# A two-layer graph network on one core: issue order written out by hand, masks on GpSimd, a per-node stage in small portions

## The chip, the core and the metric

The kernel runs on one core of a Trainium2 chip. A core has five engines that run side by side and wait for one another through semaphores: TensorE (PE, matmuls; its weight loads are listed apart as PEld), VectorE (DVE), ScalarE (ACT), GpSimd (POOL) and SyncE (SP, which here only issues DMAs). The metric is the device time of one execution in microseconds (us), the median over several runs.

## What is computed

There are N = 3327 nodes with D = 64 features and a 0/1 adjacency of 3327 x 3327. Both layers start with a layer norm and a relu and are added to their input. Cut to what matters:

```python
# layer 0: h = relu(layernorm(x)); c = 1 / r**2
left, right = x_t @ w_att[:D], x_t @ w_att[D:]             # x_t = logmap0(h)
adj_att   = sigmoid(left[:, None] + right[None, :] + b) * adj
x_local   = logmap(h[:, None], h[None, :], c)              # a vector for each pair
support_t = einsum('ij,ijd->id', adj_att, x_local)
x = x + proj(expmap(h, support_t, c), c)
# layer 1: h = relu(layernorm(x)); support = h @ weight
mask = (adj != 0); rank = cumsum(mask, axis=1)
k    = minimum(deg, 100); pos = rank - (deg - k)           # deg = rank[:, -1]
w    = mask * where(pos > 0, 0.5 ** (k - pos), 0)          # the last 100 neighbours
x = x + w @ support + bias
```

The vector of a pair is a combination of h of node i and h of node j, with a factor that depends on one scalar of the pair. So the kernel forms, for each pair, a scalar q by matmul, two gelus of it, a sigmoid, and their product with the adjacency; one matmul then sums over j. Layer 1 needs for each pair the number of neighbours behind j in row i; the weight is a power of two of that number.

## The kernel before

Nodes are padded to 26 blocks of 128. The first stage works per node (layer norm, norms, factors, 16-bit splits, and the transposes that give `ju` and `jz`, the two operands of the pair scalars). Then come the **pair stages**: four strips of columns i (8, 8, 6 and 4 blocks), and in each strip a loop over the blocks j from 25 down to 0. A **round** handles one j (in the last strip two), so that a tile has 128 rows j and 1024 columns i (768 in the third strip). There are 26 + 26 + 26 + 13 = 91 rounds. A round does, in the order of the code:

- one DMA of adjacency, `ad`, on SP's queue;
- `mask` from `ad` by a comparison on DVE (L824);
- **the count**: matmuls with the constants `ca` and `cb` (L829, L830) add to `pc`, which stays in PSUM for the whole strip; a first matmul of one row (L808) sets the offset. ACT (L834) or DVE (L836) reads `pc` into `behind`, an 8-bit array that is kept. DVE does every second read in the first strip and every fourth one later;
- tanh on ACT for the sigmoid (L841), then on DVE `sg = (sg + 1) * ad` (L842, the first product);
- four 16-bit matmuls per tile into `pq` (L847, L848), two gelus on ACT, from PSUM into SBUF (L850) and in place (L851), then on DVE `s = (s + WD) * sg` (L852, the second product);
- f32 matmuls that add to `po` over the strip (L855).

At the end of a strip `po` is copied out (L861), turned by PE (L865) and copied by ACT into `agg`. Then `post`, the **node stage** of that strip, is a generator: each `next(steps)` in the rounds of the following strip issues a piece of it. It uses DVE, ACT for squares and a tanh, and three calls of `rsqrt`, each a bit trick with three Newton steps on DVE. Its last values, `s2`, are layer 1's right side. In the node stage POOL adds the bias to `x_sb` (L771). `in_range` tests that the inputs are in the range of this fast path and sets `flag`.

**Layer 1** decodes `behind` for each j into 16-bit weights `wt` (two of five on ACT, L887, the others on DVE, L889) and multiplies with `s2` into seven PSUM tiles (L894). The node stage of the last strip runs beside it, so the last four blocks come last: 28 matmuls, then a copy out, small f32 matmuls with the layer's weight (L917), an add (L919) and a DMA for each of the seven tiles.

The order of instructions on each engine isn't the order of the code: a scheduler takes all instructions that the code traces and orders them for each engine by its own cost model, within their dependencies and buffers.

Of the kernel before, what the change touches and what calls it, by code (L numbers as in the profile page):

```python
# [14 lines left out]
I32 = mybir.dt.int32  # L15
# [15 lines left out]
JH = 13  # L31

# [35 lines left out]
CNT = 127.0  # L68
# [367 lines left out]
def fast(ctx, tc, x, adj_t, r, w_att, b_att, weight, bias, out, flag):  # L436
# [33 lines left out]
    q0_c = column(Q0, "q0_c")  # L470
    ident = const.tile([P, P], F32, name="ident")
# [3 lines left out]

    cb = const.tile([P, P], BF16, name="cb")
    ca = const.tile([P, P], BF16, name="ca")
    G.memset(ca, -1.0)
    G.affine_select(out=cb, in_=ca, compare_op=ALU.is_gt, fill=0.0, base=0,
                    pattern=[[-1, P]], channel_multiplier=1)  # L480
    G.affine_select(out=cb, in_=cb, compare_op=ALU.not_equal, fill=CNT, base=0,
                    pattern=[[-1, P]], channel_multiplier=1)
    G.tensor_sub(ca, ca, cb)
    row1 = const.tile([1, P], BF16, name="row1")
    G.memset(row1, 1.0)
    rowc = const.tile([1, 512], BF16, name="rowc")
    G.memset(rowc, MAX_NEIGH - CNT)

# [13 lines left out]
    def rsqrt(pool, y, v, n):  # L502

        t = pool.tile([P, n], F32, name="rs_t")
        g = pool.tile([P, n], F32, name="rs_g")
        V.tensor_scalar(t.bitcast(I32), v.bitcast(I32), 1, None, op0=ALU.logical_shift_right)
        V.tensor_scalar(y.bitcast(I32), t.bitcast(I32), -1.0, float(0x5F3759DF), op0=ALU.mult, op1=ALU.add)
        V.tensor_scalar(g, v, -0.5, None, op0=ALU.mult)
        for _ in range(3):
            V.tensor_mul(t, y, y)  # L510
            V.tensor_mul(t, t, g)
            V.scalar_tensor_tensor(y, t, 1.5, y, op0=ALU.add, op1=ALU.mult)

    def wide(t, n):
# [4 lines left out]
    x2, bal, balm, nrm, left, right = (  # L519
        const.tile([P, NB], F32, name=n) for n in ("x2", "bal", "balm", "nrm", "left", "right"))  # L520
# [6 lines left out]

    post_pool = ctx.enter_context(tc.tile_pool(name="post", bufs=1))
# [3 lines left out]
    with tc.tile_pool(name="pre", bufs=1) as pre:  # L532
# [17 lines left out]
        rsqrt(pre, y, v, NB)  # L550
# [58 lines left out]
        rsqrt(pre, yr, x2c, NB)  # L609
# [37 lines left out]
        V.tensor_scalar(balm, bal, MIN_NORM, None, op0=ALU.max)  # L647
        V.tensor_scalar(maxnorm, absr, 1.0 - EPS_BALL, None, op0=ALU.mult)
# [11 lines left out]
    def in_range():  # L660

        st = post_pool.tile([P, 4], F32, name="st")
        t1 = post_pool.tile([P, NB], F32, name="st1")
        V.tensor_mul(t1, nrm, node)
        V.tensor_reduce(st[:, 0:1], t1, AX.X, ALU.max)
        V.scalar_tensor_tensor(t1, x2, c_c, t1, op0=ALU.mult, op1=ALU.mult)
        V.tensor_reduce(st[:, 1:2], t1, AX.X, ALU.max)
        V.tensor_mul(t1, bal, node)
        V.tensor_reduce(st[:, 2:3], t1, AX.X, ALU.max)
        V.tensor_reduce(st[:, 3:4], t1, AX.X, ALU.min)  # L670
        V.tensor_scalar(st[:, 3:4], st[:, 3:4], -1.0, None, op0=ALU.mult)
        pf = ps.tile([P, P], F32, name="pq", bufs=2)
# [3 lines left out]
        pf = ps.tile([P, P], F32, name="pq", bufs=2)  # L676
# [12 lines left out]
    def post(agg, b0, nb):  # L689
# [11 lines left out]
        sa, t0, t1, k, y2, u2, xy, rn = (small(n) for n in ("sa", "t0", "t1", "k", "y2", "u2", "xy", "rn"))  # L701
        u, w, dt = big("u"), big("w"), big("dt")
        V.tensor_mul(t0, nrm[:, bs], balm[:, bs])
        V.tensor_mul(t1, bal[:, bs], t0)
        V.tensor_mul(dt, hs, v)
        yield
        V.tensor_reduce(xy, dt, AX.X, ALU.add)
        V.scalar_tensor_tensor(sa, xy, m2c, agg[:, :, D], op0=ALU.mult, op1=ALU.add)
        V.tensor_mul(sa, sa, t0)
        yield  # L710
        V.tensor_mul(u, v, wide(t1, nb))
        yield
        V.tensor_mul(w, hs, wide(sa, nb))
        yield
        V.tensor_sub(u, u, w)
        A.activation(dt, u, AF.Square)

        V.tensor_mul(xy, xy, t1)
        V.tensor_mul(sa, sa, x2[:, bs])
        V.tensor_sub(xy, xy, sa)  # L720
        yield

        V.tensor_reduce(u2, dt, AX.X, ALU.add)
        V.tensor_scalar(t0, u2, MIN_NORM, None, op0=ALU.max)
        yield
        rsqrt(pool, rn, t0, nb)
        V.tensor_mul(t0, t0, rn)
        V.reciprocal(t1, balm[:, bs])
        V.scalar_tensor_tensor(t0, t0, sqc, t1, op0=ALU.mult, op1=ALU.mult)
        A.activation(k, t0, AF.Tanh)  # L730
        yield
        V.scalar_tensor_tensor(k, k, absr, rn, op0=ALU.mult, op1=ALU.mult)

        V.tensor_mul(y2, u2, k)
        V.tensor_mul(y2, y2, k)
        V.tensor_mul(xy, xy, k)
        V.tensor_scalar(xy, xy, m2c, -1.0, op0=ALU.mult, op1=ALU.mult)
        V.tensor_scalar(xy, xy, 1.0, None, op0=ALU.add)
        V.scalar_tensor_tensor(t0, y2, c_c, xy, op0=ALU.mult, op1=ALU.add)
        V.scalar_tensor_tensor(t1, y2, c2_c, x2[:, bs], op0=ALU.mult, op1=ALU.mult)  # L740
        V.tensor_add(t1, t1, xy)
        V.tensor_scalar(t1, t1, MIN_NORM, None, op0=ALU.max)
        V.reciprocal(t1, t1)
        V.tensor_mul(t0, t0, t1)
        V.tensor_mul(k, k, bal[:, bs])
        V.tensor_mul(k, k, t1)
        yield
        V.tensor_mul(w, hs, wide(t0, nb))
        yield
        V.tensor_mul(u, u, wide(k, nb))  # L750
        yield
        V.tensor_add(u, u, w)
        A.activation(dt, u, AF.Square)
        yield

        V.tensor_reduce(t0, dt, AX.X, ALU.add)
        V.tensor_scalar(t0, t0, MIN_NORM, None, op0=ALU.max)
        yield
        rsqrt(pool, rn, t0, nb)
        V.tensor_scalar(rn, rn, maxnorm, 1.0, op0=ALU.mult, op1=ALU.min)  # L760
        yield
        V.tensor_mul(u, u, wide(rn, nb))
        yield
        V.tensor_add(xs, xs, u)
        yield

        V.tensor_reduce(t0, xs, AX.X, ALU.add)
        yield
        V.scalar_tensor_tensor(w, wide(t0, nb), -1.0 / D, xs, op0=ALU.mult, op1=ALU.add)  # L769
        A.activation(dt, w, AF.Square)  # L770
        G.tensor_add(xs, xs, bias_b[:, None, :].to_broadcast([P, nb, D]))  # L771
        yield
        V.tensor_reduce(t0, dt, AX.X, ALU.add)
        V.tensor_scalar(t0, t0, 1.0 / D, EPS_LN, op0=ALU.mult, op1=ALU.add)
        yield
        rsqrt(pool, rn, t0, nb)
        V.tensor_scalar(rn, rn, HS, None, op0=ALU.mult)
        yield
        V.scalar_tensor_tensor(w, w, 0.0, wide(rn, nb), op0=ALU.max, op1=ALU.mult)
        A.copy(s2[:, bs, 0], w)  # L780
        yield
        V.tensor_sub(s2[:, bs, 1], w, s2[:, bs, 0])  # L782


    steps = iter(())
    for b0, nb in STRIPS:
        F = nb * P
        i0 = b0 * P
        hv = halves(F)
        blocks = slice(b0, b0 + nb)  # L790
        queue = nc.scalar if b0 == 0 else nc.sync
# [7 lines left out]
        izf, iuf = iz.rearrange("p b q -> p (b q)"), iu.rearrange("p b q -> p (b q)")  # L799
        pc = ps.tile([P, FMAX], F32, name="pc")  # L800
        po = ps.tile([P, FMAX], F32, name="po")
        pl = ps.tile([P, FMAX], F32, name="pq", bufs=2)
        for b in range(nb):
            T.transpose(pl[:, b * P : (b + 1) * P], left[:, b0 + b : b0 + b + 1].to_broadcast([P, P]), ident)
        left_b = strip.tile([P, FMAX], F32, name="left_b", bufs=1)
        A.copy(left_b[:, :F], pl[:, :F])
        for f0, f1 in hv:
            T.matmul(pc[:, f0:f1], row1, rowc[:, : f1 - f0], start=True, stop=True, skip_group_check=True)  # L808

        per = FMAX // F  # L810
        before = None
        for hi in range(NB, 0, -per):
# [4 lines left out]
            def part(t, j, a=0, b=F):  # L817
                return t[:, (j - lo) * F + a : (j - lo) * F + b]
# [157 lines left out]
```

## Time and profile before

| | us |
|---|---|
| four runs | 459.07, 459.94, 460.09, 463.27 (median 460.01) |
| the profiled execution | 458.3 |
| its span on the core | 456.6 |
| first stage (to the first product, L842) | 0 to 47.8 |
| strips 0, 1, 2, 3 (each to the copy of `po`, L861) | 95.4, 103.9, 83.1, 57.9 |
| layer 1 to the last values of `s2` | 388.1 to 434.7 |
| last matmuls, closes, end | 434.7 to 456.6 |

A group of the profile names the line, the engine and the operation, then output and inputs with shapes (partitions x elements), how often it ran, its busy time and the mean of one. After the second bar stands how long its engine was idle just before it, and what it waited for. Busy times of an engine don't count its overlaps twice, but the durations of two instructions in a row overlap by up to a tenth of a microsecond, so a row's mean is a little more than what the instruction takes from its engine. The slices of the page give the course of things: DVE and the clock that PE is granted.

```profile
DVE  3895689999997999999998999999999999999821
ACT  1445989999894999999995999999599997888310
POOL 6000000000000000001000000010000000000000
PEclk9997699999999999999999999999999999799776
```

Each of the 40 digits is a slice of 11.4 us, in tenths of busy time, or of full clock.

### The profile page before, as it was taken

Reading aid. Unit: us, or ns where it says so; the run is one execution under the profiler, and the core shown is the slowest. Engines: PE = TensorE matmul, PEld = TensorE weight load, DVE = VectorE, ACT = ScalarE, POOL = GpSimd, SP = SyncE. Lnnn points to the kernel's source line nnn. Section 1 sums busy time; section 2 is a strip of 40 time slices with the busy share of each in tenths; the row PEclk is TensorE's granted clock in tenths of the full one; section 3 lists DMA queues with packets and bytes.
Section 4 is the critical chain, followed back from the end, with each engine's and each line's share of the span. In section 5 each row is a group of like instructions: output and inputs, shape, how many; then the busy total and the mean of one; then the engine's idle time right before and its main releaser. Section 6 shows DMA issues by size and latency. Waiting matters only on the chain.

```text
span 456.6 us, 4636 instructions
## 1 busy us (share of the span) xinstructions
PE 375.8 (82%) x1460; PEld 153.1 (34%) x1484; DVE 406.9 (89%) x774; ACT 369.2 (81%) x423; POOL 13.3 (3%) x30
## 2 busy tenths in 40 slices
PE   0266699999989799999998898898888897599392
PEld 0035233333333233333333343443333232244152
DVE  3895689999997999999998999999999999999821
ACT  1445989999894999999995999999599997888310
POOL 6000000000000000001000000010000000000000
PEclk9997699999999999999999999999999999799776
DMA  7103354545541354444443345344623430000003
GB/s 198 67 1 73 104 167 145 143 139 178 148 144 59 105 171 132 146 139 139 129 110 103 108 138 159 101 118 138 184 67 119 137 92 1 1 1 1 0 3 79
DMA packets 22840, 47.77 MB, mean 105 GB/s; under 512 B 8652, under 2 KB 9082, under 8 KB 22808
## 3 DMA queue, kind: packets, MB, share of 16 engines
q1 hardware_dynamic: 20522, 46.47, 34.7%
q10 hardware_dynamic: 2062, 0.87, 0.9%
q0 software_dynamic: 224, 0.07, 0.3%
q8 instruction: 13, 0.21, 0.2%
q14 instruction: 19, 0.16, 0.1%
HBM read 45.22 MB, written 0.85 MB: 101 GB/s over the span
## 4 chain that ended last, share of the span: by engine, by line


## 5 line engine op out<-in xcount | busy, mean ns | idle before, releaser
L855 PE MATMUL po<-s,hw 128*65 128x512 f32 (+1 forms) x364 | 164.4, 573 | 11.4 <-DVE s L852 10.7
L842 DVE SCALAR_TENSOR_TENSOR sg<-sg,ad 128x1024 f32<-128x1024 f32 (+1 forms) x91 | 103.5, 1141 | 7.5 <-ACT sg L841 7.4
L852 DVE SCALAR_TENSOR_TENSOR s<-s,sg 128x1024 f32<-128x1024 f32 (+1 forms) x91 | 104.9, 1152 | 3.7 <-ACT s L851 3.6
L841 ACT ACTIVATE sg<-left_b,right 128x1024 f32<-128x1024 f32 (+2 forms) x104 | 103.3, 1007 | 0.1
L851 ACT ACTIVATE s<-s 128x1024 f32<-128x1024 f32 (+1 forms) x91 | 92.1, 1013 | 0.1
L850 ACT ACTIVATE s<-pq 128x1024 f32<-128x1024 f32 (+1 forms) x91 | 88.3, 975 | 2.7 <-PE pq L848 2.7
L855 PEld LDWEIGHTS po<-s,hw 128*65 128x65 f32 x364 | 44.9, 137 | 98.5 <-issue 52.2
L847 PE MATMUL pq<-iu,ju 71*128 71x512 f16 (+1 forms) x182 | 67.8, 374 | 11.9 <-ACT s L850 11.6
L829 PE MATMUL pc<-mask,ca 128*128 128x512 bf16 (+1 forms) x168 | 62.5, 372 | 17.3 <-DVE behind_hi L836 6.5
L848 PE MATMUL pq<-iz,jz 128*128 128x512 f16 (+1 forms) x182 | 66.7, 372 | 0.1
L830 PE MATMUL pc<-mask,cb 128*128 128x512 bf16 (+1 forms) x169 | 61.8, 374 | 5.5 <-DVE mask L824 5.0
L824 DVE TENSOR_SCALAR mask<-ad 128x1024 bf16<-128x1024 f32 (+1 forms) x91 | 59.2, 654 | 2.7 <-PE pc L829 1.6
L834 ACT ACTIVATE behind_hi<-pc 128x1024 uint8<-128x1024 f32 (+2 forms) x37 | 32.1, 868 | 23.8 <-PE pc L830 23.6
L894 PE MATMUL pw<-wt,s 128*128 128x512 bf16 (+1 forms) x178 | 41.0, 392 | 12.3 <-DVE s L782 8.1
L830 PEld LDWEIGHTS <-cb 128*128 128x128 bf16 x182 | 17.8, 98 | 56.5 <-issue 45.4
L834 ACT ACTIVATE behind_lo<-pc 128x1024 uint8<-128x1024 f32 (+2 forms) x33 | 28.2, 853 | 5.3 <-PE pc L830 4.7
L894 PEld LDWEIGHTS <-s 128*128 128x128 f16 x182 | 18.8, 104 | 34.4 <-issue 9.6
L848 PEld LDWEIGHTS <-jz 128*128 128x128 f16 x182 | 18.1, 99 | 31.7 <-issue 15.5
L829 PEld LDWEIGHTS <-ca 128*128 128x128 bf16 x175 | 17.4, 100 | 30.4 <-issue 19.2
L847 PEld LDWEIGHTS <-ju 71*128 71x128 f16 x182 | 18.2, 100 | 21.4 <-issue 4.8
L836 DVE TENSOR_SCALAR behind_lo<-pc 128x1024 uint8<-128x1024 f32 (+2 forms) x19 | 19.9, 1050 | 0.0
L771 POOL TENSOR_TENSOR x_sb<-x_sb,bias_b 128x512 f32<-128x512 f32 (+2 forms) x4 | 6.3, 1583 | 416.2 <-DVE w L769 416.2
(209 smaller groups left out, 290.3 us busy)
## 6 DMA issues: line engine op xcount, KB each, us to landing
ad<-in_adj_t SPq DMA_DIRECT2D x65, 512.0 KB, 3.6
ad<-in_adj_t SPq DMA_DIRECT2D x26, 384.0 KB, 3.2
out<-o SPq DMA_DIRECT2D x6, 128.0 KB, 2.0
x_sb<-in_x SPq DMA_DIRECT2D x1, 416.0 KB
x_sb<-in_x ACTq DMA_DIRECT2D x1, 416.0 KB, 6.3
iz<-jz ACTq DMA_DIRECT2D x2, 128.0 KB
iz<-jz SPq DMA_DIRECT2D x2, 128.0 KB, 2.9
iz<-jz SPq DMA_DIRECT2D x2, 96.0 KB
```

The lines of the kernel that those rows point to most:

```text
L829: T.matmul(pc[:, f0:f1], ca, before[:, f0:f1], start=False, stop=True, skip_group_check=True)
L830: T.matmul(pc[:, f0:f1], cb, now[:, f0:f1], start=False, stop=True, skip_group_check=True)
L834: A.activation(kept, pc[:, :F], AF.Relu)
L841: A.activation(part(sg, j), left_b[:, :F], AF.Tanh, bias=right[:, j : j + 1], scale=0.5)
L842: V.scalar_tensor_tensor(sg[:, :span], sg[:, :span], 1.0, ad[:, :span], op0=ALU.add, op1=ALU.mult)
L847: T.matmul(part(pq, j, f0, f1), ju[:KB, j, :], iuf[:, f0:f1], start=True, stop=False)
L848: T.matmul(part(pq, j, f0, f1), jz[:, j, :], izf[:, f0:f1], start=False, stop=True)
L850: A.activation(s[:, :span], pq[:, :span], AF.Gelu, scale=-WG / QS)
L851: A.activation(s[:, :span], s[:, :span], AF.Gelu, scale=WH)
L852: V.scalar_tensor_tensor(s[:, :span], s[:, :span], WD, sg[:, :span], op0=ALU.add, op1=ALU.mult)
L855: T.matmul(po[: D + 1, f0:f1], hw[:, j, :], part(s, j, f0, f1), start=j == NB - 1, stop=j == 0)
L894: T.matmul(pw[n], s2[:, j].rearrange("p c d -> p (c d)"), wt[:, f0:f1].bitcast(BF16), start=j == 0, stop=j == NB - 1)
```

## The change

1. **Order.** The pair stages are written as functions of a round number `n` (0 to 90, over all strips) and issued under `tc.manual_schedule` for PE, DVE and ACT, so that these three keep the order of the code. Adjacency is loaded five rounds ahead (seven buffers in place of four), masks and counts run three rounds ahead, the pair scalars (`products`) one, and the sums (`total`) two behind. A round begins with its two gelus. POOL and SP are still ordered by the scheduler.
2. **Masks** are made on POOL, as 1 where there is no edge (`is_equal` 0). `ca` and `cb` are changed to fit, the offset that depends on j comes in when `pc` is read (`none`), and the matmul of one row goes. The reads are shared out between ACT and DVE by `ON_ACT` (ACT has 1/5, 4/7, 2/3 and 1/2 of them in the four strips, and all of the first three).
3. **Gelus** both run in place in PSUM; the second product reads `pq` there, and writes over `sg`, which goes into the sums. The buffers of `s` are gone.
4. **Left values** as a row on all partitions: for the first strip by transposes as before, for the others by a DMA from a copy in DRAM (`left_d`).
5. **Node stage.** It is written anew: norms are worked out from inner products of `h` and `v`, so fewer wide operations are left (12 in place of 17 on DVE, and 59 small ones in place of 65). `rsqrt` becomes a `pow` on POOL with one Newton step on DVE. Each `yield` now follows one instruction (or two) and says how much it counts; `advance` issues 2, 5, 5 and 16 units in a round of the four strips, 6 for each j of layer 1. `LATER` ends a portion, after a step of POOL or ACT.
6. **Layer 1** keeps the order of the code too. Every second decode is on ACT (13 of 26; it was 11). POOL adds the bias here. `in_range` ends here, its first part runs as node-stage steps in strip 0. The closes of the seven tiles stand between the last matmuls, two tiles behind.

```diff
+IN_ORDER = {mybir.EngineType.PE, mybir.EngineType.DVE, mybir.EngineType.Activation}
+AHEAD = 3
+SGB, ADB = 5, 7
+ON_ACT = ((1, 5), (4, 7), (2, 3), (1, 2))
+PORTIONS, LAST = (2, 5, 5, 16), 6
+BIG, LATER = 4, 99
...
-    G.memset(rowc, MAX_NEIGH - CNT)
+    G.iota(none_i, pattern=[[-P, NB]], base=MAX_NEIGH - P + 1, channel_multiplier=1)
+    G.tensor_copy(none, none_i)
...
+        if power:
+            G.tensor_tensor(y, v, nhalf[:, :n], op=ALU.pow)
+            V.tensor_scalar(g, v, -0.5, None, op0=ALU.mult)
+            yield LATER
...
+        for _ in range(1 if power else 3):
             V.tensor_mul(t, y, y)
+            yield 1
...
+        A.activation(u, v, AF.Square)
         V.tensor_mul(dt, hs, v)
+        yield BIG
+        V.tensor_reduce(hv, dt, AX.X, ALU.add)
+        yield BIG
+        V.tensor_reduce(vv, u, AX.X, ALU.add)
+        yield BIG
...
         A.activation(k, t0, AF.Tanh)
+        yield LATER
...
+    def edges(n):
+        mask_of[n] = mask = work.tile([P, FMAX], BF16, name="mask", bufs=3)
+        args = mask[:, : span(n)], ad_of[n][:, : span(n)]
+
+        G.tensor_scalar(*args, 0.0, None, op0=ALU.is_equal)
+
+    def count(n, j):
...
+        now = part(n, mask_of[n], j)
+        for f0, f1 in S.hv:
+            if not S.first:
+                T.matmul(S.pc[:, f0:f1], ca, S.before[:, f0:f1], start=False, stop=True, skip_group_check=True)
+            T.matmul(S.pc[:, f0:f1], cb, now[:, f0:f1], start=S.first, stop=True, skip_group_check=True)
+        S.before, S.first = now, False
+
+    def read(n, j):
...
+        if (n < AHEAD and k == 0) or i * num // den != (i + 1) * num // den:
+            A.activation(kept, S.pc[:, : S.F], AF.Relu, bias=rest)
+        else:
+            V.tensor_scalar(kept, S.pc[:, : S.F], rest, 0.0, op0=ALU.add, op1=ALU.max)
...
+    def sigmoids(n):
...
+            A.activation(part(n, sg, j), S.left[:, : S.F], AF.Tanh, bias=right[:, j : j + 1], scale=0.5)
...
+    with tc.manual_schedule(engines=IN_ORDER):
+        products(0)
+        for n in range(R):
+            k, lo, hi = rounds[n]
+            m, w = n + AHEAD, span(n)
...
+                load(m + 2)
+            two = m < R and len(js(m)) == 2
+            if two:
+                count(m, js(m)[0])
+            if turned:
+                pa = turn(k - 1)
+            elif n > 1:
+                total(n - 2)
+            pq = pq_of.pop(n)[:, :w]
+            A.activation(pq, pq, AF.Gelu, scale=-WG / QS)
+            A.activation(pq, pq, AF.Gelu, scale=WH)
+            if n == 0:
+                first_left()
+                sigmoids(0)
+            elif n == 1:
+                left_to_dram()
+            if turned:
+                steps = per_node(k - 1, pa)
+            sg = sg_of[n][:, :w]
+            V.scalar_tensor_tensor(sg, sg, 1.0, ad_of.pop(n)[:, :w], op0=ALU.add, op1=ALU.mult)
+            if m + 1 < R:
+                edges(m + 1)
+            if two:
+                read(m, js(m)[0])
+            if m < R:
+                count(m, js(m)[-1])
+            if n + 1 < R:
+                sigmoids(n + 1)
+            if m < R:
+                read(m, js(m)[-1])
+            if n + 1 < R:
+                products(n + 1)
+            advance(PORTIONS[k])
...
+            V.scalar_tensor_tensor(sg, pq, WD, sg, op0=ALU.add, op1=ALU.mult)
+            if turned:
+                total(n - 2)
...
-            if j % 5 < 2:
+            if j % 2:
                 A.activation(wt, behind(j), AF.Copy, scale=128.0)
...
         for j in range(late):
             wt = decode(j)
+            advance(LAST)
+            if j == 8:
+                in_range(l1_ps)
             for n in range(len(chunks)):
                 add(j, wt, n)
-            for _ in range(2):
-                next(steps, None)
+            if j % 4 == 3:
+                bias(j - 3, 4)
...
+        for n in range(len(chunks)):
+            for j in range(late, NB):
+                add(j, weights[j - late], n)
+            if n % 2:
+                A.copy(ow[n], pw[n])
+            else:
+                V.tensor_copy(ow[n], pw[n])
+            if n > 1:
+                close(n - 2)
```

In the changed kernel the first product stands at L1058, the second at L1077, the reads at L967 (ACT) and L969 (DVE), the gelus at L1048 and L1049, the mask at L944, the decodes at L1100 and L1102.

## The prediction, written before the changed kernel ran

> **What bounds the kernel now.** I read the busy table first, then the same table cut at the ends of the strips (the DVE copy at L861 starts at 143.2, 247.1, 330.2 and 388.1 us), then the groups by shape, then single instructions in order of time. The page's chain of waits is empty for this run, so the bound is read from the stages.
>
> ```profile
> PE 375.8 (82%) x1460; PEld 153.1 (34%) x1484; DVE 406.9 (89%) x774; ACT 369.2 (81%) x423; POOL 13.3 (3%) x30
> ```
>
> Cut at the strips' ends (after the length of a stretch stand the busy us of PE, weight load, DVE, ACT and POOL; the last numbers are clock, DMA share and GB/s):
>
> ```profile
> 143.20:247.10 103.90, 96.10 (x326) 34.37 (x332) 101.25 (x176) 97.14 (x105) 2.20 (x1) 1.00 0.44 129
> 247.10:330.20 83.10, 73.44 (x320) 33.70 (x323) 81.14 (x167) 76.84 (x105) 2.40 (x1) 1.00 0.46 130
> 330.20:388.10 57.90, 49.16 (x163) 17.02 (x165) 56.19 (x125) 52.50 (x78) 1.01 (x1) 1.00 0.28 83
> 388.10:434.70 46.60, 33.62 (x154) 15.93 (x158) 43.82 (x101) 34.18 (x18) 0.72 (x1) 0.86 0.00 1
> ```
>
> And the three costly groups on DVE, by shape (busy us and mean ns, then the idle time before them):
>
> ```profile
> L852 DVE SCALAR_TENSOR_TENSOR s<-s,sg 128x1024 f32<-128x1024 f32 x65 | 79.7, 1226 | 3.7 <-ACT s L851 3.6
> L842 DVE SCALAR_TENSOR_TENSOR sg<-sg,ad 128x1024 f32<-128x1024 f32 x65 | 79.0, 1217 | 7.5 <-ACT sg L841 7.4
> L824 DVE TENSOR_SCALAR mask<-ad 128x1024 bf16<-128x1024 f32 x65 | 44.9, 694 | 2.4 <-PE pc L829 1.6 <-DMA ad<-in_adj_t 0.6 <-remote 0.2
> ```
>
> In strips 1 to 3 DVE is busy 97% of the time (101.25 of 103.9), ACT 91 to 93%, PE 85 to 92%. DVE is the bound, but the next two are so near that relief of DVE is soon capped. POOL is idle.
>
> Instructions overlap their neighbours, so I count start to start:
>
> ```profile
> 162.48 1.22 DVE L852 SCALAR_TENSOR_TENSOR s<-s,sg 128x1024 f32<-128x1024 f32 x1 [0.22 <-ACT s L851]
> 163.62 1.22 DVE L842 SCALAR_TENSOR_TENSOR sg<-sg,ad 128x1024 f32<-128x1024 f32 x1
> 164.76 1.22 DVE L836 TENSOR_SCALAR behind_hi<-pc 128x1024 uint8<-128x1024 f32 x1
> ```
>
> and on ACT:
>
> ```profile
> 157.56 1.08 ACT L851 ACTIVATE s<-s 128x1024 f32<-128x1024 f32 x1
> 158.50 1.17 ACT L841 ACTIVATE sg<-left_b,right 128x1024 f32<-128x1024 f32 x1
> 159.54 1.05 ACT L850 ACTIVATE s<-pq 128x1024 f32<-128x1024 f32 x1
> 160.45 1.06 ACT L834 ACTIVATE behind_hi<-pc 128x1024 uint8<-128x1024 f32 x1
> ```
>
> A DVE product or read of 1024 takes 1.13 of DVE's time, a mask 0.60 (L824 to L842 at 149.53 and 150.13), an ACT gelu 0.90 or 0.94, a tanh 1.04, a read on ACT 0.90. PE needs 0.215 for each half of 512 in 16 bits (eight in a round) and 1.72 for the four f32 ones (L855 at 153.24, next matmul at 154.96): 3.44 us in a round of 1024.
>
> **What the Trainium skill says.** "SBUF — State Buffer", section "Who interferes with whom": GpSimd shares a port pair with DVE, exclusively and for a whole instruction; a DVE operation with two SBUF inputs contends with a GpSimd one that reads SBUF, and so does a 2-port mode; one with a PSUM source does not. The trace agrees. POOL's bias add (L771) runs alone in 0.72 (256 elements) and 1.01 (384). When it holds the port, DVE is late:
>
> ```profile
> 380.61 1.01 POOL L771 TENSOR_TENSOR x_sb<-x_sb,bias_b 128x384 f32<-128x384 f32 x1 [71.56 <-DVE w L769]
> 381.04 1.65 DVE L852 SCALAR_TENSOR_TENSOR s<-s,sg 128x1024 f32<-128x1024 f32 x1
> ...
> 306.64 2.40 POOL L771 TENSOR_TENSOR x_sb<-x_sb,bias_b 128x512 f32<-128x512 f32 x1 [89.06 <-DVE w L769]
> ```
>
> L852 takes 1.65 in place of 1.22. At 306.64 the reverse: POOL waits through L842 and a mask on DVE, and gets in only when DVE reaches a one-input reduce. "GPSIMD Engine Reference", section "Performance versus the Vector engine", gives 1.03 to 2.6 cycles per element at 1.2 GHz. "ScalarE: Activation LUTs", section "What ACT_TABLE_LOAD costs": a pointer bias adds 93 ns; the trace has 1176 (tanh, bias) against 1078 (gelu, none).
>
> **The change, part by part.**
>
> *Masks to GpSimd.* DVE loses 65 x 0.60 + 26 x 0.47 = 51 us. The trace has no comparison on POOL. Its two-input adds give 2.21 ns per element and 0.16 fixed (1.01 less 0.72 over 128). Its cast of 128x128 took 0.293: with 0.16 fixed, 1.04 ns per element and 1.22 us for 1024; with 0.10 fixed (a 128x1 memset), 1.64. From the skill's bounds, with 0.16, 1.04 to 2.38. I take 1.4 (1.1 for 768). POOL itself has room: one mask a round, started when PE has finished with the buffer three masks back, needed about a round later. The price is the port. The first product (now L1058) and the node stage's small operations use it; the second product (now L1077, its gelu in PSUM) and the count reads do not. POOL gets in when one of those starts and holds on 1.4 - 1.13 = 0.27 too long. Ends: 0 to 1.25. I take 0.2 a round in strips 1 to 3, nothing in strip 0, where DVE has slack.
>
> *Gelus back to back.* The second gelu now needs the first directly before it, in place. No row shows such a pair; I add 0.05 to a full duration: 1.09 in place of 0.90, so a round is 1.09 + 0.90 + 1.04 = 3.03 on ACT, and 1.0 for a read there (0.90 and the bias). Lower end: no wait, 0.15 a round less.
>
> *Node stage in portions.* DVE goes from 17 wide operations and 65 small ones a strip to 12 and 59. Wide: 0.61 at 512. Small: 0.08 apart where others stand between (158.00 against 157.92), 0.20 in a chain (386.34, 386.55, 386.75); in portions they are a chain. So 12 x 0.61 + 59 x 0.20 = 19.1 us, against about 17 x 0.61 + 65 x 0.1 = 17: no gain.
>
> *Rounds*, the engine that ends last decides:
> - Strip 0: PE 3.44; DVE 2.26 + 4/5 x 1.19 = 3.21; ACT 3.03 + 0.20 = 3.23. I take 3.45.
> - Strip 1: DVE 2.26 + 3/7 x 1.19 + 19.1/26 + 0.2 = 3.70; ACT 3.03 + 4/7 x 1.0 + 0.1 (2.8 us of the node stage) = 3.70. Before 103.9/26 = 4.00.
> - Strip 2 (768): DVE 1.74 + 0.31 + 0.73 + 0.2 = 2.98; ACT 0.86 + 0.72 + 0.81 + 0.53 + 0.11 = 3.03; PE 2.58. Before 3.20.
> - Strip 3: DVE 2.26 + 0.67 + (12 x 0.48 + 59 x 0.20)/13 + 0.2 = 4.48 in ten rounds, 3.3 in the last three, which have no count; ACT 4.0. Before 4.45.
>
> *Start.* Before, the first gelu stands at 49.1: behind left's transposes, copy, two table loads of 1.28 and a tanh. Now it needs only the first products, whose last load is issued at 40.6. DVE before that sheds 4 masks (2.4), two reads (2.3) and the range check's start (0.9), and gains four small operations and waits on POOL's first masks: about 3.5 earlier. First tanh about 45, first second product done at 47.4, against 53.5 (L852 at 52.34). PE's clock is 0.67 between 40 and 60 us: 3 us more.
>
> *Sum to the last copy out of PSUM:* 47.4 + 25 x 3.45 + 3 + 26 x 3.70 + 26 x 3.03 + 54.7 + three copies out of 1.13 + 2.0 for the last totals = 371.7, against 388.1.
>
> *Layer 1.* Before: 46.6 us until the last node values, bound by DVE (43.8 busy), then 14.0 for the last 28 matmuls (7.87, slow clock) and the closes, then 7.9 after the last add. After: ACT takes 13 decodes in place of 11: 13 x 2.92 = 38, with 1.8 of small work, after 2.1 us for the turn and the first copies; it stands in front of the tanh (idle about 2.5 us, decode 5 queued behind) and of the square (4). That is 48.5. DVE: 13 x 1.81 + 5 + 12 + waits, about 44 with 2 for the waits on PE and ACT, plus up to 7 x 0.7 if POOL's bias adds (0.72 each) take the port during decodes. The closes now run between the last matmuls: 28 x 0.215 + 52 x 0.114 + 1 = 12.9. Sum 48.5 + 12.9 + 7.9 = 69.3 against 68.5. No gain, ends 64 and 74.
>
> *At nothing:* seven row matmuls gone (2.5 on PE, at strip starts); three broadcast reads of left on SP's queue, 1.2 MB among 46, behind adjacency loads that land in 3.6 us and are issued five rounds ahead; pow on POOL, queued behind at most one mask there and hidden on DVE by the product or decode that follows each portion: with a mask of 1.4 ahead and over 1 us of its own it would show, three times a strip. The range check's steps lie in strip 0, where DVE has 0.2 a round to spare; its end, in layer 1, has DVE wait twice for PE transposes queued behind the matmuls, some 1 to 2 us that ACT's 48.5 covers.
>
> Span 371.7 + 69.3 = 441.0 against 456.6. The profiled run took 458.3, 1.7 over its span, so 442.7; the median of the runs is 460.0, 1.7 above the profiled run: **444.4**.
>
> **Rivals.**
> - *Floor:* no port waits, gelus as close as before. 3.55, 2.90 and 4.28 a round in strips 1 to 3: 26 x 0.15 + 26 x 0.13 + 10 x 0.2 = 9 us less, 435. For it: POOL has two PSUM operations a round to hide under. Against: nothing in the trace shows that a gelu can start on the result of the one before it without a wait.
> - *The port becomes the bound:* masks at 2 cycles per element, 1.93 us, hold DVE 0.8 a round; 0.6 x 62 rounds above my 0.2: 482. It ends slower than before once the wait passes 0.2 + 15.5/62 = 0.45 us, a mask of 1.58. For it: the 1.65 above. Against: the cast's 0.293.
> - *Given back in hand-overs:* in a fixed order each of six ACT or POOL steps of a strip may stop DVE; 6 x 4 x 0.3 = 7 us, and 5 more in layer 1: 456, about no change.
> - That masks stay on DVE can be excluded: all 91 are issued on POOL.
>
> **Chances.** Forecast 0.58, floor 0.18, port 0.13, hand-overs 0.11. 429 to 463 leaves out the port case and a little below the floor. Faster by over 1% (below 455.4): most of the first, all of the second, a little of the last, 0.78; within 1%, about what a measurement can tell: 0.09; slower 0.13.
>
> **What would show it.** POOL busy about 91 x 1.3 = 120 us. L1058 long (above 1.3) in some rounds, L1077 at 1.22 always. Strip 1 near 96 us, strip 0 near PE's 3.44. First gelu near 41. Gelu pairs 1.1 apart. ACT idle in front of the tanh in layer 1. Masks above 1.6 us, or L1058 near 2, would make it wrong.

## The result, and the profile after

The changed kernel takes 458.65 us (median of 32 runs, 455.26 to 461.63), the kernel before 460.67 (53 runs, 458.30 to 464.38): a ratio of 0.9959, 95% interval 0.9942 to 0.9975. Forecast were 444.4. The profiled span is 452.7 us, against 456.6. The profiled executions took 454.55 and 458.30 us, 4.1 and 2.4 below their kernels' medians, so a difference of a few us between two traces need not be one between the kernels.

The busy table of the page of the changed kernel:

```profile
PE 364.5 (81%) x1442; PEld 154.4 (34%) x1460; DVE 393.3 (87%) x660; ACT 369.4 (82%) x399; POOL 289.0 (64%) x137
```

POOL is busy 289 us, 253.7 of them with masks, where about 120 were expected, and DVE has lost only 13.6 of its 406.9. The groups by shape name the two operations (after the bar: busy us, mean ns of one, then idle time before them):

```profile
L944 POOL TENSOR_SCALAR mask<-ad 128x1024 bf16<-128x1024 f32 x65 | 193.7, 2985 | 62.6 <-PE pc L955 50.7 <-remote 5.2 <-issue 2.5
L944 POOL TENSOR_SCALAR mask<-ad 128x768 bf16<-128x768 f32 x26 | 60.0, 2312 | 18.4 <-PE pc L956 13.3 <-PE pc L955 3.9 <-POOL mask L944 1.2
...
L1058 DVE SCALAR_TENSOR_TENSOR sg<-sg,ad 128x1024 f32<-128x1024 f32 x65 | 85.5, 1315 | 6.2 <-ACT sg L976 6.2
L1077 DVE SCALAR_TENSOR_TENSOR sg<-pq,sg 128x1024 f32<-128x1024 f32 x65 | 79.1, 1217 | 2.4 <-ACT pq L1049 1.3
```

A mask takes twice the 1.4 us of the prediction. The first product (L1058, both inputs in SBUF) is 0.1 longer in the mean than the second (L1077, its gelu in PSUM), which never takes longer than 1.23. Single instructions of POOL, and then of DVE over the same microseconds, show how the 0.1 comes about:

```profile
154.92 2.77 POOL L944 TENSOR_SCALAR mask<-ad 128x1024 bf16<-128x1024 f32 x1 [0.68 <-PE pc L955]
158.38 6.22 POOL L944 TENSOR_SCALAR mask<-ad 128x1024 bf16<-128x1024 f32 x2 [0.69 <-PE pc L955]
```

```profile
156.30 0.16 DVE L746 TENSOR_TENSOR sa<-sa,su 128x8 f32<-128x8 f32 x1
156.38 0.16 DVE L749 TENSOR_TENSOR xy<-hv,sv 128x8 f32<-128x8 f32 x1
...
157.99 1.22 DVE L1058 SCALAR_TENSOR_TENSOR sg<-sg,ad 128x1024 f32<-128x1024 f32 x1
159.13 1.00 DVE L757 TENSOR_TENSOR t<-sa,hv 128x8 f32<-128x8 f32 x1
160.16 0.17 DVE L759 TENSOR_TENSOR u<-u,t 128x8 f32<-128x8 f32 x1
...
161.86 2.08 DVE L1058 SCALAR_TENSOR_TENSOR sg<-sg,ad 128x1024 f32<-128x1024 f32 x1
```

The mask at 154.92 meets no obstacle: 2.77 us. After 158.38 two follow each other in 6.22: the first is held up, and two operations of DVE are late in the same stretch, the product at 161.86 (2.08 in place of 1.22) and, where nobody would look, an operation of 128x8 at 159.13 (1.00 in place of 0.17).

But a mask doesn't keep DVE out for all of its 2.77 us. The operations at 156.30 and 156.38 have two SBUF inputs each, run while the mask of 154.92 is still at work, and take their usual 0.16. Of the 206 operations with two SBUF inputs that overlap a mask in this trace, 37 are longer than usual, by at most 0.88 us where the mask has 1024 columns and by at most 0.63 where it has 768. That is about 0.85 ns a column, less than a third of the mask's own time, and it falls at the mask's beginning.

Cut at the copies out of PSUM (L999 starts at 143.46, 246.18, 334.75 and 389.66; after the length of a stretch stand the busy us of PE, weight load, DVE, ACT and POOL):

```profile
143.46:246.18 102.72, 91.53 (x310) 34.18 (x315) 98.39 (x136) 92.63 (x99) 79.08 (x31) 0.98 0.42 126
246.18:334.75 88.57, 74.56 (x320) 34.28 (x319) 82.50 (x137) 79.74 (x106) 72.17 (x32) 0.98 0.45 129
334.75:389.66 54.91, 43.19 (x134) 15.29 (x134) 49.17 (x104) 43.03 (x59) 25.67 (x12) 0.97 0.16 48
```

DVE is still busy 96% of strip 1. The last copy comes at 389.66 (before 388.10, forecast 371.7), so the main loop has gained nothing; what is left of the gain is layer 1, 63.0 us in place of 68.5. (In thirteen traces with this layer 1 and this node stage, this one and twelve of the experiments', it takes 62.9 to 66.8.)

### The profile page after: what moved, and what is told of

Same layout as the page of the kernel before. It is cut to its first block, busy times and chain, and to the rows that moved or that the text cites. A ratio compares the mean times of both kernels' runs of the same rounds, so it can differ in the third digit from the quotient of the medians.

```text
span 452.7 us, 4813 instructions
## 1 busy us (share of the span) xinstructions
PE 364.5 (81%) x1442; PEld 154.4 (34%) x1460; DVE 393.3 (87%) x660; ACT 369.4 (82%) x399; POOL 289.0 (64%) x137
## 4 chain that ended last, share of the span: by engine, by line
PE 35%; DVE 30%; ACT 21%; issue 8%; DMA 2%; POOL 2%; another core or an unknown queue 0%; ACTq 0%; DVEq 0%; POOLq 0%
PE po L993 15%; DVE sg L1077 7%; DVE sg L1058 7%; ACT pq L1048 5%; PE pq L983 5%; ACT wt L1100 4%; ACT sg L976 4%; PE pq L984 4%; PE pc L956 4%; PE pc L955 3%; ACT pq L1049 3%; DVE behind_lo L969 2%; PE pw L1107 2%; DMA w_lr<-in_w_att 2%; DVE behind_hi L969 1%
## 5 line engine op out<-in xcount | busy, mean ns | idle before, releaser
L944 POOL TENSOR_SCALAR mask<-ad 128x1024 bf16<-128x1024 f32 (+1 forms) x91 | 253.7, 2793 | 81.0 <-PE pc L955 54.7
L993 PE MATMUL po<-sg,hw 128*65 128x512 f32 (+1 forms) x364 | 162.9, 571 | 1.6 <-DVE sg L1077 1.3
L1058 DVE SCALAR_TENSOR_TENSOR sg<-sg,ad 128x1024 f32<-128x1024 f32 (+1 forms) x91 | 112.7, 1238 | 6.2 <-ACT sg L976 6.2
L1077 DVE SCALAR_TENSOR_TENSOR sg<-pq,sg 128x1024 f32<-128x1024 f32 (+1 forms) x91 | 103.8, 1141 | 2.6 <-ACT pq L1049 1.3
L1048 ACT ACTIVATE pq<-pq 128x1024 f32<-128x1024 f32 (+1 forms) x91 | 86.7, 952 | 21.2 <-PE pq L984 19.9
L1049 ACT ACTIVATE pq<-pq 128x1024 f32<-128x1024 f32 (+1 forms) x91 | 86.2, 947 | 3.0
L956 PE MATMUL pc<-mask,cb 128*128 128x512 bf16 (+1 forms) x179 | 65.3, 375 | 13.2 <-POOL mask L944 11.2
L993 PEld LDWEIGHTS po<-sg,hw 128*65 128x65 f32 x364 | 50.2, 140 | 73.7 <-issue 57.2
L969 DVE TENSOR_SCALAR behind_lo<-pc,none 128x1024 uint8<-128x1024 f32 (+2 forms) x26 | 29.0, 1115 | 5.0 <-ACT pq L1049 2.6
L969 DVE TENSOR_SCALAR behind_hi<-pc,none 128x1024 uint8<-128x1024 f32 (+2 forms) x26 | 28.2, 1085 | 5.2 <-PE pc L956 4.9
L967 ACT ACTIVATE behind_lo<-pc,none 128x1024 uint8<-128x1024 f32 (+2 forms) x26 | 23.9, 919 | 7.5 <-PE pc L956 5.1
L517 POOL TENSOR_TENSOR rn<-t,nhalf 128x8 f32<-128x8 f32 (+2 forms) x8 | 13.7, 1710 | 25.1 <-DVE t L770 22.4
L967 ACT ACTIVATE behind_hi<-pc,none 128x1024 uint8<-128x1024 f32 (+2 forms) x26 | 24.5, 943 | 6.1 <-PE pc L956 3.9
```

Of the source, the lines that this page charges most:

```text
L944: G.tensor_scalar(*args, 0.0, None, op0=ALU.is_equal)
L956: T.matmul(S.pc[:, f0:f1], cb, now[:, f0:f1], start=S.first, stop=True, skip_group_check=True)
L969: V.tensor_scalar(kept, S.pc[:, : S.F], rest, 0.0, op0=ALU.add, op1=ALU.max)
L993: T.matmul(S.po[: D + 1, f0:f1], hw[:, j, :], part(n, sg_of[n], j, f0, f1), start=j == NB - 1, stop=j == 0)
L1048: A.activation(pq, pq, AF.Gelu, scale=-WG / QS)
L1049: A.activation(pq, pq, AF.Gelu, scale=WH)
```

## The experiments

Each is the changed kernel with one edit, except the fourth; where masks go back to DVE, the reads are divided anew as well. The ratios are to the kernel before, timed beside them (medians of 459.8 to 460.9), with the 95% interval in brackets. The medians are of 4 runs; every second mask, the Newton steps, the division of decodes and the fourth buffer alone have 20.

**No masks in the loop.** `mask_of[n] = same`, a tile of zeros made once, so that the count counts no real edges.

> The changed kernel with one mask of zeros, made once, for every round, so that the counting has no real masks and nothing of them is made in the loop; all else and its order stay. Theory A (the GpSimd mask gives the saving back): the whole price of the mask goes, its lateness and its port: strip 1 falls from 102.7 us to about 92, the first product to 1.22 us always, and the time to 430 to 438 us. Theory B (hand-overs of the fixed order): within 1% of the changed kernel, 454 to 463 us. Theory C (18 more reads on DVE give it back): also near the changed kernel, 450 to 458.

Measured: 437.14 us, ratio 0.950 (0.9474 to 0.9527). Rounds are 3.68 us in strip 1 and 3.01 in strip 2, counted from first product to first product, where the changed kernel has 4.03 and 3.30. The GpSimd mask costs about 21 us, with the hand-overs and the 18 additional reads on DVE all in place: theories B and C fall as the main cause. Strips 1 and 2 cut as above:

```profile
141.26:235.13 93.87, 89.82 (x308) 34.53 (x315) 88.20 (x136) 91.20 (x99) 6.37 (x5) 0.98 0.46 137
235.13:315.73 80.60, 72.39 (x315) 33.83 (x319) 73.61 (x137) 78.95 (x106) 7.16 (x5) 1.00 0.50 141
```

DVE issues the same 660 instructions as in the changed kernel, 136 and 137 of them here, and is busy 10.2 us less in strip 1 and 8.9 less in strip 2; the strips are 8.9 and 8.0 us shorter. So what DVE waits in these strips comes out, nearly us for us, as time. Over the whole span the difference in busy time is 23.4 us (393.3 and 369.9).

**The mask at the price that the prediction gave it.** Only the first 512 columns are compared, and the count uses them for all columns.

```
-        args = mask[:, : span(n)], ad_of[n][:, : span(n)]
+        args = mask, ad_of[n][:, :512]
```

> The changed kernel with the GpSimd mask made of the first 512 columns alone and used for all columns of the count, so that the mask takes about half: 1.4 to 1.5 us, the price that the prediction assumed. Theory A says that the size of the mask was the failing term: 440 to 448 us, the forecast of the record. If the length matters less than that a port is asked for at all (theory A2): 450 to 456. Theory B (hand-overs): within 1% of the changed kernel, 454 to 463.

Measured: 440.73 us, ratio 0.9576 (0.9548 to 0.9603). The groups by shape of this run:

```profile
L944 POOL TENSOR_SCALAR mask<-ad 128x512 bf16<-128x512 f32 x91 | 161.9, 1781 | 154.4 <-PE pc L955 95.4 <-PE pc L956 27.8 <-remote 16.0
...
L1058 DVE SCALAR_TENSOR_TENSOR sg<-sg,ad 128x1024 f32<-128x1024 f32 x65 | 79.4, 1222 | 6.8 <-ACT sg L976 6.8
```

The mask takes 1.49 us where nothing holds it up (1.78 in the mean), and the first product is back at 1.22. The edit cuts two things at once, how long GpSimd works and how many columns it reads: the longest wait of an operation with two SBUF inputs is now 0.42 us. The next run parts the two.

**As long on GpSimd, but nothing read.** The mask is replaced by memsets of 1024, 1024 and 640 columns (768, 768 and 480 in strip 2).

> The changed kernel with each mask written by three memsets on GpSimd (1024, 1024 and 640 columns, about 2.7 us together by the 1.05 us of one in the run without masks), so that GpSimd works as long as in the changed kernel but reads nothing from SBUF; the counting gets masks of zeros. Port theory (the mask costs what DVE waits for the port that a reading GpSimd operation holds): first products stay at 1.22 us, DVE busy about 370 to 375 us, time 436 to 443. Lateness theory (the mask costs because a GpSimd engine 2.8 us long hands it over too late): DVE busy also about 375, but PE waits for the mask and the time stays at 452 to 460.

Measured: 439.02 us, ratio 0.9499 (0.9424 to 0.9574). A round's memsets take 2.65 us in strip 1 from the first start to the last end (the median), nearly as long as a mask, and the first product doesn't notice; groups by shape:

```profile
L944 POOL MEMSET mask<- 128x1024 bf16 x130 | 123.4, 952 | 77.6 <-PE pc L955 74.2
...
L1058 DVE SCALAR_TENSOR_TENSOR sg<-sg,ad 128x1024 f32<-128x1024 f32 x65 | 79.3, 1220 | 6.3 <-ACT sg L976 6.3
```

DVE issues the same 660 instructions as in the changed kernel and is busy 374.7 us in place of 393.3. The 18.6 between them are waits that are there only while GpSimd reads SBUF. This is what the Trainium skill states ("SBUF — State Buffer", section "Who interferes with whom": two SBUF inputs contend with a GpSimd instruction that reads, not with one that only writes): no operation with two SBUF inputs waits for a memset in this trace. So it is not that a mask of 2.8 us comes late: it is what it holds. PE's waits say the same. In the changed kernel, and here, PE waits for a mask once, 11.2 us for the very first, and never in the loop.

The memsets aren't free all the same: DVE is busy 4.8 us more than without masks. What waits here are operations with one input, from SBUF to SBUF, some twenty of them. One takes 0.80 in place of 0.17 and ends with a pair of memsets, at 191.0:

```profile
190.20 0.80 DVE L833 TENSOR_SCALAR y<-y 128x8 f32<-128x8 f32 x1
```

```profile
189.02 1.96 POOL L944 MEMSET mask<- 128x1024 bf16 x2 [0.80 <-PE pc L955]
```

**The mask alone, in the kernel before.** `V.tensor_scalar(mask..., not_equal)` becomes `G.tensor_scalar(mask..., is_gt)`.

> The kernel before with this one edit: its masks are made on GpSimd (a greater-than in place of the not-equal), all else left to the planner as it was. Theory A: DVE sheds 51 us of masks but waits for the port, and the mask of 2.77 us is late: within 1.5% of before, 454 to 467 us, POOL busy 250 us. Theory B: the port hardly matters, so relief of the engine that is busy 97% shows: 435 to 447 us.

Measured: 492.43 us, ratio 1.0719 (1.0682 to 1.0756): worse than either theory. Here the second product (L852) reads its gelu from SBUF, so both products contend. Groups by shape, and then DVE in order of time:

```profile
L852 DVE SCALAR_TENSOR_TENSOR s<-s,sg 128x1024 f32<-128x1024 f32 x65 | 92.1, 1418 | 9.7 <-ACT s L851 9.6
L842 DVE SCALAR_TENSOR_TENSOR sg<-sg,ad 128x1024 f32<-128x1024 f32 x65 | 88.3, 1363 | 14.3 <-ACT sg L841 14.3
```

```profile
165.63 2.06 DVE L842 SCALAR_TENSOR_TENSOR sg<-sg,ad 128x1024 f32<-128x1024 f32 x1
167.61 1.21 DVE L836 TENSOR_SCALAR behind_hi<-pc 128x1024 uint8<-128x1024 f32 x1
168.75 1.67 DVE L852 SCALAR_TENSOR_TENSOR s<-s,sg 128x1024 f32<-128x1024 f32 x1
```

Between them the read of PSUM (L836) takes its usual 1.21. DVE is busy 410.6 us, more than before, though it makes no masks. It is also idle 77.6 us where it was 49.7, so longer operations on DVE aren't the whole loss; how much the planner's order adds was not separated. In the changed kernel the second product keeps its 1.22 because its gelu stays in PSUM, so the move of the masks leans on that other part of the change; how much of the 34 us between the two kernels is due to it was not tried.

**All masks back on DVE**, with the reads divided as before (`ON_ACT = ((1, 2), (3, 4), (3, 4), (3, 4))`).

> The changed kernel with its masks back on DVE and the count reads divided as before (half on ACT in strip 0, three quarters after). The mask in the changed kernel's trace takes 2.77 us on GpSimd, twice the 1.4 of the prediction. Theory A (that mask and the SBUF port it holds give the saving back): no port waits on DVE, whose work is about that of before (393 less 15 of waits, less 21 for 18 reads, plus 51 = 408 us), while the start (6 us) and layer 1 (5.5 us) stay gained: 445 to 453 us, faster than the changed kernel. Theory B (the fixed order's hand-overs between PE, ACT and DVE give it back, the port hardly matters): DVE has more work in the same order, so slower than the changed kernel: 462 to 475 us.

Measured: 454.04 us, ratio 0.9874 (0.9845 to 0.9904). This is below the changed kernel's whole interval and just above the upper end of theory A; theory B's 462 and more does not come. The order, the start, the node stage and layer 1 gain 1.3%; the move of the masks, with the division of reads that goes with it, gives back 0.9% of the time.

**Half of each mask on either engine, and every second mask on either.** Strip 0 stays on GpSimd, and a few more reads are on ACT.

> The changed kernel with each mask of strips 1 to 3 made in two halves, one on GpSimd and one on DVE (strip 0 stays whole on GpSimd), and a few more count reads on ACT (5 of 8 and 3 of 4 in strips 1 and 2). Port theory: a half takes 1.4 us on GpSimd and hardly delays DVE, which pays 0.34 us for its own half: 443 to 450 us, faster than the changed kernel and than the one with all masks on DVE (454.0). If asking for the port at all costs more than the half saves: 452 to 460.

> The same split of the work in time in place of columns: in strips 1 to 3 every second mask whole on GpSimd and every second whole on DVE, reads as in the run with halves. Port theory: half of the whole masks' waits stay (7 of 14 us) and DVE pays 0.60 us in every second round: 445 to 453 us, a little slower than with halves. Lateness theory: GpSimd has two rounds for one mask, so nothing is late and it is faster than halves or equal: 440 to 447.

Measured: 455.94 (ratio 0.9868, 0.9787 to 0.9950), in the range for the case that asking for the port costs more than the half saves, and 460.26 us (0.9980, 0.9952 to 1.0008), outside both ranges. The group of DVE's masks in the second shows why:

```profile
L944 DVE TENSOR_SCALAR mask<-ad 128x1024 bf16<-128x1024 f32 x20 | 23.1, 1154 | 0.0
```

Where DVE makes all of them, one takes 0.69. A mask on DVE, too, waits for GpSimd's (by up to 0.89 us), and to divide the masks puts one more operation in its way.

**GpSimd masks in strip 0 only**, then also more reads on ACT.

> The changed kernel with its masks on GpSimd in strip 0 alone and on DVE in strips 1 to 3, reads there three quarters on ACT. Port theory: strip 0 has no node stage, its round (3.46 to 3.52 us in every run) is PE's and the port has room there, so nothing is lost by a GpSimd mask and the rest is as with all masks on DVE (454.0): 451 to 454 us, faster than both kernels. If strip 0 pays for the port too: 455 to 459.

> As the run with GpSimd masks in strip 0 alone, with 4 of 5 reads of strip 1 and 6 of 7 of strip 2 on ACT. If DVE still bounds those strips, 2 reads a strip less on it give 3 to 4 us: 448 to 451. If ACT's three functions and a read (3.03 and 0.8 us of a 3.9 us round) are by now as long: no change or slower, 452 to 457.

Measured: 453.03 (0.9848, 0.9773 to 0.9923), as the port theory had it, and 452.50 us (0.9829, 0.9756 to 0.9903), in the range for no gain from more reads on ACT. The latter is the lowest of the kernels that make every mask, and faster than both kernels: its interval lies below the changed kernel's. Their intervals and that of all masks on DVE overlap, so between these three nothing is decided. That strip 0 has room is shown: its round is 3.48 and 3.51 us with GpSimd masks, 3.48 with DVE's.

**Shorter holds.** Two GpSimd operations a mask, then four, then four or one with a fourth mask buffer.

> The changed kernel with each whole mask made by two GpSimd operations of at most 512 columns in place of one. If the length of one hold of the port is what DVE pays (the run with one piece of 1.4 us left the first products at 1.22): 444 to 451 us. If the sum of the holds in a round is what counts (two pieces of 1.4 us, 2.8 in all, beside the first product's 1.13 and the node stage's small operations, in a round of 4 us): no gain, 455 to 462.

> The changed kernel with each mask made by GpSimd operations of 256 columns, four in place of one (by 2.77 us for 1024 and 1.4 for 512 about 0.7 each, 2.9 a round). Hold-length theory (DVE pays for the rest of the hold that it runs into): its busy time falls on, from 386 us with two pieces to 378 to 382, and the time to 446 to 451. Sum-of-holds theory (GpSimd now waits for DVE and is late): the time stays with the two pieces, 452 to 457, and PE waits for masks.

> Masks in four pieces and a fourth mask buffer, so that GpSimd may start a round earlier (the adjacency tiles get six buffers in place of seven, for room). If with short holds only lateness is left: 441 to 448 us. If the port is short in the sum: 450 to 456, no better than the pieces alone.

> The changed kernel with whole masks and a fourth mask buffer (the adjacency tiles six in place of seven). Port theory: DVE waits as before for holds of 2.8 us, 455 to 461 us. Lateness theory (GpSimd sat 55 us before its masks waiting for PE to free a buffer): 446 to 453.

Measured: 453.35 (ratio 0.9848, 0.9774 to 0.9922), 477.37 (1.0325, 1.0265 to 1.0384), 477.83 (1.0343, 1.0282 to 1.0404) and 462.97 us (1.0047, 1.0022 to 1.0073). Two pieces lie between their two expectations: DVE is busy 386.4 us, so 6.9 us of its waits are gone, and the strip 1 round is 3.94. Both runs with four pieces miss: DVE waits hardly less (busy 385.8 us with four pieces alone), and now POOL is the bound, busy 105.5 of the 106.3 us of strip 1. From the groups by shape of the run with four pieces, and then from its waits (us in total, times, longest us):

```profile
L944 POOL TENSOR_SCALAR mask<-ad 128x256 bf16<-128x256 f32 x338 | 340.3, 1034 | 19.3 <-issue 16.4 <-POOL mask L944 1.8 <-DMA ad<-in_adj_t 1.1
```

```profile
PE pc L956 <- POOL mask L944: 32.2, 21, 12.7
```

Four at 1.03 make 4.1 us, more than a round, and PE waits 19.5 us for masks in the loop, where it waited for none (the 12.7 are the wait for the very first mask); even strip 0 goes from 3.49 to 3.95 a round. A piece that meets nothing takes 0.84, so 0.2 of it is fixed. The last run is above both its ranges, and whether a fourth buffer alone helps can't be read from it: it took an adjacency buffer for it, and GpSimd then waited 83 us for adjacency loads.

**Powers and decodes.**

> The changed kernel with the three inverse square roots of the node stage by three Newton steps on DVE in place of a power on GpSimd and one step. It takes 12 powers of 1.3 to 2.0 us (21 us) from GpSimd and gives DVE 96 small operations of about 0.12 us (11 us). If the powers matter by the port they hold: 450 to 456 us, faster than the changed kernel. If they are hidden, as the prediction has it, DVE's 11 us count where DVE is the bound: 457 to 465.

> The changed kernel with layer 1's decodes divided as before (two of five on ACT in place of every second). If the division made layer 1's gain of 5.5 us over the kernel before: DVE's 24 us of decodes become 28 to 30, the time grows by 3 to 5 us, to 461 to 464. If the order of the last sums and closes made it (the last copy out of PSUM to the last decode was 46.6 before and 45.5 after, the rest 21.9 and 17.5): within 1.5 us of the changed kernel, 457 to 460.

Measured: Newton steps 466.25 us (1.0108, 1.0079 to 1.0136), just above the range for hidden powers, and the old division of decodes 462.80 (1.0054, 1.0032 to 1.0076), in its first range. DVE is busy 12.6 us more with Newton steps and the time grows by 7.6, so the powers are worth their place on GpSimd. With two of five decodes on ACT layer 1 takes 462.2 - 393.2 = 69.0 us, about the 68.5 of before; with every second it takes 63.0 in the changed kernel, up to 66.8 in the other traces. The last decode ends 50.7 us after the last copy in place of 45.4. So the division makes layer 1's gain, though its size, 2 to 6 us, differs from trace to trace.

## Why the prediction was wrong

*Masks to GpSimd, "I take 1.4", and from it "I take 0.2 a round".* This is the step that failed: the price of a GpSimd mask, in its length and in what DVE waits for it. The mask takes 2.77 us for 1024 and 2.12 for 768 where it meets nothing, above 2.38, the higher end of the prediction's estimate. With 1.49 for 512 and 0.84 for 256 this is 0.2 fixed and 2.5 ns an element; I had 0.16 fixed and at most 2.2, and took my value from a cast of 128 columns. A cast is no comparison, and 128 columns say little on a slope. The page "GPSIMD Engine Reference", section "Performance versus the Vector engine", has 1.03 to 2.6 cycles an element at 1.2 GHz; 2.5 ns are 3.0 of such cycles, so the measurement lies outside and decides. Its section "Engine selection" calls operations of one input roughly line-rate; here DVE does the mask in 0.60, GpSimd in 2.77. The prediction had named its own sign, "masks above 1.6 us, or L1058 near 2": both came.

DVE's waits, as its busy time above that of the run without masks, are 10.2, 8.9 and 2.0 us in strips 1 to 3: 0.39, 0.34 and 0.15 a round, where 0.2 was taken for all. From the end of the first second product to the last copy out of PSUM the changed kernel takes 338.7 us, where 324.3 were forecast and the run without masks takes 319.4.

With the mask of 512, whose length is the assumed one, most of the rest of the working stands. Rounds in us, from first product to first product:

| strip | predicted | mask of 512 | changed kernel |
|---|---|---|---|
| 0 | 3.45 | 3.52 | 3.49 |
| 1 | 3.70 | 3.71 | 4.03 |
| 2 | 3.03 | 3.08 | 3.30 |
| 3 | 4.48, then 3.3 | 4.54 mean | 4.67 mean |

The four strips together, counted as above, take 323.8 us with the mask of 512 (predicted 324.3). Strip 3 is the exception: by the prediction the mean of its twelve intervals would be 4.28, and even without masks it is 4.50. That the time, 440.7, is near the 444.4 is luck in part, for two errors work against each other: the start comes 3.2 us later than forecast, and layer 1 is 4.1 shorter. The rest of the mask costs 458.65 - 440.73 = 17.9 us. Whether a mask of 1024 columns that took 1.4 us would also have left DVE waiting is not shown, since no run has one.

*What a hold of the port costs, "holds on 1.4 - 1.13 = 0.27 too long".* The mechanism, that DVE's operations with two SBUF inputs wait for GpSimd, is right; the rule for the size is wrong. By it a mask of 2.77 would hold DVE 2.77 - 1.13 = 1.64 us in each round, and the kernel would be slower by far. The rule took a hold for the whole instruction, as the page that the prediction names has it, and let every hold end in a first product. In the trace before, the wait of 0.43 at 381.04 ended near the end of a two-input add, so it looked so. Beside masks a wait of an operation with two SBUF inputs ends within 0.88 us for 1024 columns, a third of the mask; there page and measurement differ, and the measurement decides. Such a hold is shorter than the 1.13 of a read or second product, and only 15 of 91 first products are above 1.3 us. What makes up for it is the number of those that wait. That DVE's small operations would pay was said; they make nearly half (12 us, the first products 9). The mask of 512 costs DVE 379.0 - 369.9 = 9.1 us in all, not 0.2 x 65 = 13. POOL waits in its turn (masks of 2985 ns in the mean), but PE never waits for a mask in the loop.

*What DVE gained.* 51 us of masks went and 18 reads more at 1.19 came (21); without masks in the loop DVE is busy 369.9, so the other parts take off some 7 more. Of these 37 us the masks on GpSimd give back 23.4 as waits: the 13.6 of the table.

*Gelus back to back, 1.09.* Right within 0.05: they start 1.04 apart (42.85 and 43.89).

*Start.* The first gelu came at 42.85 (predicted 41, before 49.1), the first second product ended at 50.9 (predicted 47.4, before 53.5): less than half of the gain. Without masks in the loop they are 41.23 and 49.3, so the masks take 1.6 us of it; what takes the rest was not tried.

*Node stage and powers.* "No gain" from portions wasn't tested alone. That powers would "show, three times a strip" above 2 us is not seen: the powers of 128x8 take 1.75 and 2.04 us in the mean, and the first step after them (L526) 0.51 in place of the 0.17 of the next step (L528), some 2 us over the six of them. But the three that are long start within 0.7 us of the start of a mask, and their waits, 0.63 to 0.84 us, are those of a mask.

*Layer 1, 69.3, "no gain".* Mis-sized by 2.5 to 6.4: 63.0 in the changed kernel, 65.2 with the mask of 512, up to 66.8 in other traces. The waits that were foreseen on ACT are there, in order of time:

```profile
400.08 0.20 ACT L777 ACTIVATE k<-t 128x4 f32<-128x4 f32 x1 [2.62 <-DVE t L775]
...
417.17 0.42 ACT L856 ACTIVATE dt<-w 128x256 f32<-128x256 f32 x1 [2.55 <-DVE w L854]
```

but the terms were too long: the decodes end after 45.4 us (predicted 48.5), the last sums after 11.0 more (12.9), the tail takes 6.6 (7.9). Of these only the first is steady; with the mask of 512 the other two are 12.7 and 7.1.

*Rivals.* "The port becomes the bound" named the mechanism and gave it 0.13; with its price of a hold corrected it is what happened, and ends at about no change rather than at 482. (Its 1.93 us for 2 cycles an element are 1.87 by the 0.16 that the prediction takes as fixed.) The hand-overs (456) gave a time close to the measured one for another reason; without masks the same order takes 437.

## What to carry to other kernels

Before work is moved to GpSimd, find its duration there for that very operation and size, or treat it as unknown; a cast of another size is no price for a comparison. Then count the port: how many columns GpSimd reads, which of DVE's operations have two SBUF inputs, small ones too, and whether they fall at the beginning of such a read. In this case an operation that only writes didn't hold up any of those, and a product with one input in PSUM never waited; one-input operations from SBUF to SBUF waited for both kinds.

## What the runs showed of the hardware that was not expected

A GpSimd comparison, float32 to bfloat16, costs 2.5 ns an element and 0.2 us, 4.6 times DVE's. DVE operations of eight elements wait for the port as long as large ones do (0.84 us in an operation of 128x8, 0.88 in a product of 128x1024).

The wait goes with the columns that GpSimd reads and not with the whole length of its operation. The longest of an operation with two SBUF inputs is 0.88, 0.63, 0.42 and 0.26 us beside masks of 1024, 768, 512 and 256 columns, which take 2.77, 2.12, 1.49 and 0.84; later in a mask such operations run at their usual length. One-input operations from SBUF to SBUF wait at the end of a mask as well: one of 128x8 at 180.59 in the changed kernel takes 0.75 in place of 0.17 and ends with the mask, at 181.3.

Two pieces of 512 gain 5 us over one of 1024, four of 256 lose 19: of the three sizes that were tried the middle one is best, between holds that are too long and a sum that is too long.
